# The second residual added with tokens along the partitions, instead of through the down product

## The chip, the cores and the metric

The kernel runs on one core of one Trainium2 chip. The metric is the device time of one execution in microseconds; the figure given for a kernel is the median of its runs. Engines are named as in the profile: PE is TensorE's matrix product, PEld its loading of weights, DVE is VectorE, ACT ScalarE, POOL GpSimd, and SP the queue that issues most DMAs. Each engine works through its own list of instructions in the order in which the program wrote them.

## The reference

The input `x` has 16 sequences of 256 tokens with 128 features, float32. Twelve layers of linear attention (16 heads of 8 features, no softmax) with residuals come first, then two post-norm steps, the second around a gated feed-forward network whose weights are integers times 1/127:

```python
for i in range(12):
    q, k, v = split(x @ Wqkv[i].T + bqkv[i])
    att = einsum('bhqd,bhkd->bhqk', q, k) / sqrt(8)
    x = einsum('bhqk,bhkd->bhqd', att, v) @ Wproj[i].T + bproj[i] + x
x1 = layernorm(x0 + x)                       # x0: the input
gate, up = x1 @ (w_gate / 127).T, x1 @ (w_up / 127).T      # 384 hidden features
out = layernorm(x1 + (silu(gate) * up) @ (w_down / 127).T)
```

`layernorm` takes off the mean and divides by sqrt(variance + 1e-5), with no weights. The change concerns the last line.

## The kernel before

The 16 sequences are worked on as 8 pairs (`p`) of 512 tokens, in two halves of four pairs for the attention. The attention never forms tokens: it carries a 128 x 128 matrix per sequence through the layers and multiplies the tokens by it at the end. Then `ffn(p, prio)` does the rest for one pair:

- `tr_t`, `tr_c`, `mm_r`: the carried matrix is transposed and multiplied with the pair's tokens, which gives `x0 + x` with tokens along the partitions, four chunks of 128 tokens (K = 4) side by side in one PSUM bank.
- `norm(pr, True)`: first norm, from that bank into the SBUF tile `x1` (its memory is that of `kv`, so the profile writes `kv`). The mean is already off; the sum of squares comes from ScalarE (L588) or VectorE (L591, L593).
- `tr_x`: four transposes (L655) bring `x1` into a bank with features along the partitions. There it is split in two parts of reduced precision, `xh` (L657) and the rest `xl` (L658), because products in that precision run faster.
- For each of three blocks of 128 hidden features: gate and up products on `xh` and `xl` (L665, L666), Silu on ScalarE (L668), gate times up on VectorE (L669), the split of the result in `hh` (ScalarE or VectorE) and `hl` (GpSimd or VectorE), and the down products on `hh` and `hl` (L677, L678), which add up in one bank `pd` over the three blocks. `sg0` is written into `xt`, `sg1` into `qgv`.
- The second residual comes in two parts. `xl` enters the bank `pd` as a product with 127 times the identity (`id127r`, L676), and `xh` is added on VectorE as the bank is read: `sg0 = pd / 127 + xh` (L680).
- `tr_o`: four transposes (L684) turn `sg0` back to tokens along the partitions, in bank `po`.
- `norm(po, False)`: second norm, read from that bank. Statistics on VectorE (four L591, four L593), then on GpSimd variance + eps (L600) and its power -0.5 (L601), then `nb` = -mean * rs (L619), then the scaling of four chunks on VectorE (L613) or ScalarE (L615) into the memory of `x1`, and the store (L688). The bank `po` is held until the scaling is done.

Copies, subtractions and casts go through helpers, so many of them have lines L199 (ScalarE), L201 (VectorE or GpSimd) and L204 (subtractions on either).

The order on each engine is not written by hand. Every step is handed to `plan.op(costs, emit, reads, writes, prio)` with a price in ns for each engine that may do it. `Plan.run` is a list scheduler: for every step that is ready it finds the engine on which it would end first, takes the steps that could start earliest, and among these the one with the smallest `prio` less 0.0001 times the price of the longest way that follows it. Pair `p` of the feed-forward part has `prio` 11 + 0.15 p. A step that needs one of the 8 PSUM banks waits until one is free in the plan. So prices decide both the engine and the order. Those that matter here are 69 + n/0.96 for VectorE (n elements per partition), 51 + n/1.2 for ScalarE reading a bank and 94 + n/1.2 reading SBUF, 93 more for each pointer operand; 1276 for the second norm's scaling on VectorE (K * 319); 2.6 N for the store.

At the start, before the plan, GpSimd and VectorE make constants one after another: the identity, masks, `center`, `ones`, and `id127` (L250) with its cast `id127r` (L251). Behind them GpSimd sets the columns of ones beside the loaded tokens (L266), for which TensorE's first products (L329) wait.

Of the kernel before, what the change touches and what calls it, by code (L numbers as in the profile page):

```python
# [9 lines left out]
F32 = mybir.dt.float32  # L10
F32R = mybir.dt.float32r
BF16 = mybir.dt.bfloat16
I32 = mybir.dt.int32
AF = mybir.ActivationFunctionType
ALU = mybir.AluOpType
# [6 lines left out]
C = 128  # L22
# [6 lines left out]
QSCALE = 1.0 / 127.0  # L29
# [5 lines left out]
N = PB * T  # L35
K = N // 128
# [33 lines left out]
PE, ACT, DVE, POOL, SP = "pe", "act", "dve", "pool", "sp"  # L70
# [95 lines left out]
def mmr(n):  # L166
    return max(111, 0.447 * n + 5)


def act(n, sbuf=False, pointers=0):  # L170
    return (94 if sbuf else 51) + 93 * pointers + n / 1.2


def dve(n, fast=False):
    return 69 + n / (1.92 if fast else 0.96)
# [11 lines left out]
def linear_attention_ffn_kernel(ctx: ExitStack, tc: tile.TileContext, x, xt, wall, wq0, bias, wg, wu, wd, out):  # L187
    nc = tc.nc
    sb = ctx.enter_context(tc.tile_pool(name="sb", bufs=1))
    ps = ctx.enter_context(tc.tile_pool(name="ps", bufs=1, space=PSUM))  # L190
    new = lambda name, shape, dt=F32: sb.tile([128, *shape], dt, name=name)
# [3 lines left out]
    bank = lambda v: banks[v.slot]  # L195
# [21 lines left out]
    ident = new("ident", [128])  # L217
# [19 lines left out]
    for g in range(G):  # L237
        rows = slice(32 * g, 32 * g + 32)
# [6 lines left out]
    nc.vector.tensor_copy(centerr, center)  # L245
    ones = new("ones", [C], BF16)
    nc.gpsimd.memset(ones, 1.0)

    id127, id127r = new("id127", [128]), new("id127r", [128], F32R)
    nc.gpsimd.tensor_scalar(id127, ident, 1.0 / QSCALE, 0.0, ALU.mult, ALU.add)  # L250
    nc.vector.tensor_copy(id127r, id127)  # L251


    xts = [new(f"xt{p}", [PB * T]) for p in range(NP)]
    vx = [Val() for _ in range(NP)]
# [287 lines left out]
    vfw = {n: Val() for n in "gud"}  # L543
# [7 lines left out]
    for p in range(NP):  # L551
        t = {f"{n}{j}": new(f"{n}{j}_{p}", [512], F32R) for n in ("hh", "hl") for j in range(NB)}
# [15 lines left out]
    def ffn(p, prio):  # L568
# [8 lines left out]
        def op(costs, emit, reads, writes):  # L577
            plan.op(costs, emit, reads, writes, prio)

        def norm(src, centred):  # L580

            xs, rows = t("x1"), lambda: bank(src)
            cut = lambda a, k: a[:, k * C : (k + 1) * C]

            def stats(e):
                if e == ACT:
                    for k in range(K):
                        nc.scalar.activation(cut(xs, k), cut(rows(), k), AF.Square, scale=1 / math.sqrt(C), accum_out=t("mv")[:, k, 1:2])  # L588
                else:
                    for k in range(K):  # L590
                        nc.vector.bn_stats(t("st")[:, k, :], cut(rows(), k))  # L591
                    for k in range(K):
                        nc.vector.bn_aggr(t("mv")[:, k, :], t("st")[:, k, :])  # L593
            costs = {DVE: K * (dve(C) + 70)}
            if centred:
                costs[ACT] = K * (act(C) + 93)
            op(costs, stats, [src], [v["st"], v["x1"]])

            def rstd(e):
                nc.gpsimd.tensor_scalar(t("ve"), t("mv")[:, :, 1], 1.0, EPS, ALU.mult, ALU.add)  # L600
                nc.gpsimd.tensor_tensor(t("rs"), t("ve"), mhalf, ALU.pow)  # L601
            op({POOL: 1220}, rstd, [v["st"]], [v["rs"]])

            def scale(e):
                if centred and e == DVE:
                    nc.vector.tensor_tensor(chunks(xs), chunks(rows()), t("rs").unsqueeze(2).to_broadcast([128, K, C]), ALU.mult)
                    return
                for k in range(K):
                    d, r, rs = cut(xs, k), cut(rows(), k), t("rs")[:, k : k + 1]
                    if centred:  # L610
                        nc.scalar.activation(d, r, AF.Copy, scale=rs)
                    elif e == DVE:
                        nc.vector.tensor_scalar(d, r, t("mv")[:, k, 0:1], rs, ALU.subtract, ALU.mult)  # L613
                    else:
                        nc.scalar.activation(d, r, AF.Identity, bias=t("nb")[:, k : k + 1], scale=rs)  # L615
            if centred:
                costs = {DVE: dve(N), ACT: K * act(C, False, 1)}
            else:
                op({DVE: 75}, lambda e: nc.vector.scalar_tensor_tensor(t("nb"), t("mv")[:, :, 0], -1.0, t("rs"), ALU.mult, ALU.mult), [v["rs"], v["st"]], [v["nb"]])  # L619
                costs = {DVE: K * 319, ACT: K * act(C, False, 2)}  # L620
            op(costs, scale, [src, v["rs"], v["st"], v["nb"]], [v["x1"]])


        ptt, pc, pr, px, pd, po = (Val("bank") for _ in range(6))
# [34 lines left out]
        for n in range(NH):  # L659
# [12 lines left out]

            def mm_d(e, n=n, hh=hh, hlo=hlo):
                ws = fw["d"][:, n * C : (n + 1) * C]
                if n == 0:
                    nc.tensor.matmul(bank(pd), id127r, t("xl"), start=True, stop=False)  # L676
                nc.tensor.matmul(bank(pd), ws, t(hh), start=False, stop=False)  # L677
                nc.tensor.matmul(bank(pd), ws, t(hlo), start=False, stop=(n == NH - 1))  # L678
            op({PE: (2 + (n == 0)) * mmr(N)}, mm_d, [v[hh], v[hlo], v["xl"], vfw["d"]], [pd])
        op({DVE: dve(N)}, lambda e: nc.vector.scalar_tensor_tensor(t("sg0"), bank(pd), QSCALE, t("xh").bitcast(F32), ALU.mult, ALU.add), [pd, v["xh"]], [v["sg0"]])  # L680

        def tr_o(e):
            for k in range(K):
                nc.tensor.transpose(bank(po)[:, k * C : (k + 1) * C], t("sg0")[:, k * 128 : (k + 1) * 128], ident)  # L684
        op({PE: K * 109}, tr_o, [v["sg0"]], [po])
        norm(po, False)
        r0 = p * N
        op({SP: 2.6 * N}, lambda e: nc.sync.dma_start(out[r0 : r0 + N, :].rearrange("(k p) c -> p k c", p=128), chunks(t("x1"))), [v["x1"]], [])  # L688

# [56 lines left out]
```

## Time and profile before

| | |
|---|---|
| three runs | 313.88, 314.54, 315.0 us; median 314.54 |
| profiled execution | 314.09 us, span from first to last instruction 312.4 us, mean granted TensorE clock 0.986 |
| busy time over the span | PE 297.9 us (95%), DVE 240.1 (77%), ACT 212.4 (68%), POOL 135.4 (43%) |
| chain that ended last | PE 90%, DVE 5%, POOL 2%, DMA 1% |
| first and last start of L676 (8 products of 512 columns) | 266.7 and 297.3 us |
| first and last start of L680 (8, VectorE) | 275.6 and 303.1 us |
| first and last start of L684 (32 transposes) | 279.9 and 304.5 us |
| second norm's scaling | 12 instructions on VectorE (3 pairs), 20 on ScalarE (5 pairs) |
| store of a pair's result | 256 KB, 2.3 us from issue to landing |

Shares over the whole span mix the attention, which lasts until about 254 us, with the feed-forward part behind it, where all that the change moves takes place. The busy time of PE counts a product until its modelled end, and products overlap: the distance from start to start (0.23 us for 512 columns) tells what one costs. The same holds for the four short VectorE or ScalarE instructions of a norm: a row's mean is longer than the distance.

### The profile page before, as it was taken

Reading aid. Unit: us, or ns where it says so; the run is one execution under the profiler, and the core shown is the slowest. Engines: PE = TensorE matmul, PEld = TensorE weight load, DVE = VectorE, ACT = ScalarE, POOL = GpSimd, SP = SyncE. Lnnn points to the kernel's source line nnn. Section 1 sums busy time; section 2 is a strip of 40 time slices with the busy share of each in tenths; the row PEclk is TensorE's granted clock in tenths of the full one; section 3 lists DMA queues with packets and bytes.
Section 4 is the critical chain, followed back from the end, with each engine's and each line's share of the span. In section 5 each row is a group of like instructions: output and inputs, shape, how many; then the busy total and the mean of one; then the engine's idle time right before and its main releaser. Section 6 shows DMA issues by size and latency. Waiting matters only on the chain.

```text
span 312.4 us, 12885 instructions
## 1 busy us (share of the span) xinstructions
PE 297.9 (95%) x5338; PEld 272.9 (87%) x5338; DVE 240.1 (77%) x756; ACT 212.4 (68%) x577; POOL 135.4 (43%) x228
## 2 busy tenths in 40 slices
PE   6989999999999999999999999999999999999970
PEld 6979989999999999999999999999999898888840
DVE  4768887767777677776767777676768798999995
ACT  2448796666767667676686766866876778867651
POOL 6317531445314453144531445312330357568863
PEclk9999999999999999999999999999999999999995
DMA  7473630200202102020120200310000000001124
GB/s 223 110 202 107 187 104 4 65 26 20 69 2 66 26 28 63 2 74 17 30 59 4 64 25 28 81 27 2 4 2 3 5 0 0 2 1 34 37 84 118
DMA packets 22474, 15.66 MB, mean 50 GB/s; under 512 B 1936, under 2 KB 19856, under 8 KB 22416
## 3 DMA queue, kind: packets, MB, share of 16 engines
q1 hardware_dynamic: 22128, 14.75, 17.2%
q8 instruction: 42, 0.69, 0.9%
q14 instruction: 16, 0.13, 0.1%
q10 hardware_dynamic: 288, 0.09, 0.1%
HBM read 8.02 MB, written 2.10 MB: 32 GB/s over the span
## 4 chain that ended last, share of the span: by engine, by line
PE 90%; DVE 5%; POOL 2%; DMA 1%; issue 0%; DVEq 0%; SPq 0%; POOLq 0%
PE bank L456 14%; PE bank L435 8%; PE bank L512 8%; PE bank L437 7%; PE bank L436 6%; PE bank L443 5%; PE bank L500 4%; PE bank L530 4%; PE bank L529 4%; PE bank L531 4%; PE bank L665 3%; PE bank L666 3%; PE bank L444 3%; PE bank L445 3%; PE bank L329 3%; PE bank L649 2%
## 5 line engine op out<-in xcount | busy, mean ns | idle before, releaser
L204 POOL TENSOR_TENSOR thl<-tst,thl 128x260 fp32r<-128x260 f32 x88 | 64.7, 768 | 125.4 <-ACT thl L199 125.4
L199 ACT COPY qgv<-bank 128x256 f32<-128x256 f32 x160 | 56.5, 376 | 22.5 <-PE bank L445 13.3
L199 ACT COPY kv<-bank 128x512 f32<-128x512 f32 (+1 forms) x91 | 51.8, 572 | 21.0 <-PE bank L437 15.1
L435 PE MATMUL bank<-whl,thl 128*128 128x256 f32 x176 | 51.8, 294 | 0.0
L437 PE MATMUL bank<-whl,thl 128*128 128x256 f32 x176 | 49.5, 281 | 0.0
L436 PE MATMUL bank<-whl,thl 128*128 128x256 f32 x176 | 49.4, 281 | 0.0
L456 PE MATMUL bank<-kv,g 128*128 128x128 f32 x352 | 46.3, 275 | 0.0
L536 DVE TENSOR_TENSOR tst<-bank,tst 128x260 f32<-128x260 f32 x96 | 37.0, 424 | 12.0 <-PE bank L531 9.9
L456 PEld LDWEIGHTS bank<-kv,g 128*128 128x128 f32 x352 | 42.9, 191 | 0.2 <-issue 0.2
L199 ACT CAST thl<-tst 128x260 fp32r<-128x260 f32 x88 | 33.1, 408 | 14.5 <-DVE tst L536 14.4
L449 DVE TENSOR_SCALAR qgv<-bank,bcol 128x2 f32<-128x2 f32 x88 | 19.4, 221 | 26.4 <-ACT qgv L199 22.1
L435 PEld LDWEIGHTS bank<-whl,thl 128*128 128x128 f32 x176 | 33.1, 188 | 4.3 <-issue 4.2
L525 DVE TENSOR_TENSOR yhl<-bank,yhl 128x260 fp32r<-128x260 f32 x96 | 34.1, 417 | 0.0
L436 PEld LDWEIGHTS bank<-whl,thl 128*128 128x128 f32 x176 | 33.2, 189 | 0.0
L437 PEld LDWEIGHTS bank<-whl,thl 128*128 128x128 f32 x176 | 33.1, 188 | 0.0
L443 PE MATMUL bank<-thl,whl 128*128 128x260 f32 x88 | 29.1, 330 | 0.0
L512 PE MATMUL bank<-qgv,gm 32*32 32x130 f32 x1536 | 25.8, 280 | 0.7 <-DVE gm L207 0.7
L199 ACT CAST yhl<-bank 128x260 fp32r<-128x260 f32 (+1 forms) x56 | 20.6, 412 | 7.0 <-PE bank L512 5.2
L201 DVE CAST yhl<-bank 128x260 fp32r<-128x260 f32 x48 | 18.3, 423 | 8.9 <-PE bank L512 8.8
L444 PE MATMUL bank<-thl,whl 128*128 128x260 f32 x88 | 24.8, 281 | 0.0
L445 PE MATMUL bank<-thl,whl 128*128 128x260 f32 x88 | 24.7, 280 | 0.0
L512 PEld LDWEIGHTS bank<-qgv,gm 32*32 32x32 f32 x1536 | 17.2, 103 | 6.2 <-DVE gm L207 0.9
(155 smaller groups left out, 717.4 us busy)
## 6 DMA issues: line engine op xcount, KB each, us to landing
wraw<-wall SPq DMA_DIRECT2D x12, 256.0 KB, 3.4
wpt<-whl SPq DMA_DIRECT2D x24, 96.0 KB, 2.2
qgv<-x SPq DMA_DIRECT2D x8, 256.0 KB, 5.2
xt<-xt SPq DMA_DIRECT2D x8, 256.0 KB, 4.4
out<-kv SPq DMA_DIRECT2D x8, 256.0 KB, 2.3
wpt<-whl SPq DMA_DIRECT2D x24, 64.0 KB, 2.8
wpt<-whl SPq DMA_DIRECT2D x24, 32.0 KB, 2.3
wraw<-wg SPq DMA_DIRECT2D x1, 192.0 KB, 2.8
```

Of the source, the lines that this page charges most:

```text
L199: nc.scalar.copy(dst, src)
L204: (nc.vector if e == DVE else nc.gpsimd).tensor_tensor(dst, a, b, ALU.subtract)
L435: nc.tensor.matmul(o, hi[:, b, 0:C], hl(0, 1, 2), start=True, stop=False)
L436: nc.tensor.matmul(o, hi[:, b, 0:C], hl(1, 1, 2), start=False, stop=False)
L437: nc.tensor.matmul(o, lo[:, b, 0:C], hl(0, 1, 2), start=False, stop=True)
L443: nc.tensor.matmul(o, hl(0, 0), flat(hi), start=True, stop=False)
L444: nc.tensor.matmul(o, hl(0, 0), flat(lo), start=False, stop=False)
L445: nc.tensor.matmul(o, hl(1, 0), flat(hi), start=False, stop=True)
L456: nc.tensor.matmul(bank(pgv)[:, b * C : (b + 1) * C], g0[p][:, b, :], tv(b), start=True, stop=True)
L512: nc.tensor.matmul(bank(pys[r])[group(g + r), b * W : (b + 1) * W], gm[group(g), r * PB + b, :], qss[p][group(g), b, :], start=True, stop= ...
L525: plan.op({DVE: dve(PB * W)}, lambda e: nc.vector.tensor_tensor(yl, bank(py)[:, : PB * W], yh.bitcast(F32), ALU.subtract), [py, vyh[p]], [ ...
L536: plan.op({DVE: dve(PB * W)}, lambda e: nc.vector.tensor_tensor(ts, bank(pw)[:, : PB * W], ts, ALU.add), [pw], [vt[p], vc[p]], prio)
```

## The change

The first norm's result `x1` is still in SBUF with tokens along the partitions when the second norm begins. The change adds it there:

- `id127`, `id127r` and the product L676 go; the first down product opens the bank.
- The bank `pd` is read by a scaling alone, `sg0 = pd / 127`, on ScalarE or VectorE by the plan's choice, in the place of L680.
- Behind the transposes a new VectorE addition writes `x1 = po + x1` in place.
- The second norm takes its statistics from `x1` in SBUF, and its scaling reads and writes `x1` there. The bank `po` is free after the addition.
- The prices of that scaling are changed to 4 x 190 = 760 on VectorE and to the SBUF price on ScalarE (4 x 387 = 1547 where it was 4 x 343 = 1373).

The residual is now the unsplit `x1`; the arithmetic is otherwise that of before.

```diff
-    id127, id127r = new("id127", [128]), new("id127r", [128], F32R)
-    nc.gpsimd.tensor_scalar(id127, ident, 1.0 / QSCALE, 0.0, ALU.mult, ALU.add)
-    nc.vector.tensor_copy(id127r, id127)
...
         def norm(src, centred):
-            xs, rows = t("x1"), lambda: bank(src)
+            xs = t("x1")
+            rows = (lambda: bank(src)) if src else (lambda: xs)
+            read = [src] if src else [v["x1"]]
...
-            op(costs, stats, [src], [v["st"], v["x1"]])
+            op(costs, stats, read, [v["st"], *([v["x1"]] if src else [])])
...
-                costs = {DVE: K * 319, ACT: K * act(C, False, 2)}
-            op(costs, scale, [src, v["rs"], v["st"], v["nb"]], [v["x1"]])
+                costs = {DVE: K * 190, ACT: K * act(C, True, 2)}
+            op(costs, scale, [*([src] if src else []), v["rs"], v["st"], v["nb"]], [v["x1"]])
...
             def mm_d(e, n=n, hh=hh, hlo=hlo):
                 ws = fw["d"][:, n * C : (n + 1) * C]
-                if n == 0:
-                    nc.tensor.matmul(bank(pd), id127r, t("xl"), start=True, stop=False)
-                nc.tensor.matmul(bank(pd), ws, t(hh), start=False, stop=False)
+                nc.tensor.matmul(bank(pd), ws, t(hh), start=(n == 0), stop=False)
                 nc.tensor.matmul(bank(pd), ws, t(hlo), start=False, stop=(n == NH - 1))
-            op({PE: (2 + (n == 0)) * mmr(N)}, mm_d, [v[hh], v[hlo], v["xl"], vfw["d"]], [pd])
-        op({DVE: dve(N)}, lambda e: nc.vector.scalar_tensor_tensor(t("sg0"), bank(pd), QSCALE, t("xh").bitcast(F32), ALU.mult, ALU.add), [pd, v["xh"]], [v["sg0"]])
+            op({PE: 2 * mmr(N)}, mm_d, [v[hh], v[hlo], vfw["d"]], [pd])
+        def leave(e):
+            if e == ACT:
+                nc.scalar.activation(t("sg0"), bank(pd), AF.Copy, scale=QSCALE)
+            else:
+                nc.vector.tensor_scalar(t("sg0"), bank(pd), QSCALE, None, ALU.mult)
+        op({ACT: act(N), DVE: dve(N)}, leave, [pd], [v["sg0"]])
...
         op({PE: K * 109}, tr_o, [v["sg0"]], [po])
-        norm(po, False)
+
+        op({DVE: dve(N)}, lambda e: nc.vector.tensor_tensor(t("x1"), bank(po), t("x1"), ALU.add), [po], [v["x1"]])
+        norm(None, False)
```

## The prediction

> **What bounds the kernel now.** I read the page first: the chain that ended last is 90% TensorE and 5% VectorE. Then the chain's last part in order of time, to see where the one hands over to the other:
>
> ```profile
> 293.42 0.23 PE bank L678
> 293.65 0.45 PE bank L684 x4
> 294.10 0.02 issue
> 294.12 0.68 DVE xt L669
> 294.80 0.60 DVE xt L680
> ...
> 303.15 0.60 DVE xt L680
> 303.75 0.80 DVE st L591 x4
> ```
>
> TensorE carries the end until 294.1 us; the last 15 us are VectorE's. Everything the change touches but the set-up lies after 254 us (first gate product). Busy time by stretch (columns: stretch, length, then busy us of PE, PEld, DVE, ACT, POOL, with counts):
>
> ```profile
> 280.00:285.00 5.00, 5.00 (x27) 4.11 (x26) 5.00 (x17) 3.34 (x8) 3.85 (x5) 1.00 0.00 0
> 285.00:290.00 5.00, 5.00 (x27) 4.11 (x25) 4.80 (x16) 4.16 (x11) 4.64 (x5) 1.00 0.19 52
> ...
> 300.00:305.00 5.00, 2.58 (x11) 1.32 (x9) 4.92 (x24) 1.18 (x5) 2.26 (x4) 0.88 0.54 155
> ```
>
> TensorE has no gap before 299, but VectorE has hardly one either: over the stretches from 260 to 300 (9.30 and 9.71 of 10 us, then 5.00, 4.80, 4.83 and 5.00 of 5) it idles 0.70 + 0.29 + 0 + 0.20 + 0.17 + 0 = 1.36 us. In the order of time one pair takes the same 4.85 us on both: output transposes (L684) start at 284.72 and 289.57, and the products L669 that stand at the same place of VectorE's round at 284.60 and 289.45. GpSimd's round (`hl` to `hl`, 284.31 to 289.18) is 4.87 with 0.19 idle. ScalarE alone has room, 0.82 to 0.84 a round. So less TensorE work helps only as far as the others can follow.
>
> **The change part by part.** The profiled execution took 314.09 us (span 312.4, 1.7 around it); the median of the runs is 314.54, 0.45 above. I sum changes and apply them to the median. Prices, from the groups kept apart by shape (mean ns before the last bar):
>
> ```profile
> L658 DVE TENSOR_TENSOR thl<-bank,yhl 128x512 fp32r<-128x512 f32 x8 | 5.5, 682 | 0.8 <-ACT yhl L199 0.8
> ...
> L680 DVE SCALAR_TENSOR_TENSOR xt<-bank,yhl 128x512 f32<-128x512 f32 x8 | 5.4, 677 | 0.0
> ...
> L613 DVE TENSOR_SCALAR kv<-bank,mv,rs 128x128 f32<-128x128 f32 x12 | 4.1, 400 | 0.0
> ...
> L676 PE MATMUL bank<-thl,id127r 128*128 128x512 f32 x8 | 3.4, 425 | 0.0
> ```
>
> *Set-up.* L250 on GpSimd and L251 on VectorE go. The chain runs through L250 (4.66) to the memsets (4.90) that release TensorE's first product at 5.06, so 0.24 us comes out. Bounds: 0, should the input's landing then be last, and 0.30 (the row's duration). L251 (0.80) goes at nothing: VectorE then waits 1.40 for TensorE.
>
> *The pass of 127 times the identity.* Matmuls of this shape start 0.23 us apart, so eight passes are 1.85 us of TensorE. Those at 293.84 and 297.29 lie behind the hand-over; six count, 1.39. What is late next is VectorE, with 1.36 idle, then GpSimd. Bounds 0 and 1.36. I take half, 0.70: fewer products do not speed GpSimd's round, but the two hh casts and hl subtractions a round that can sit on either of two engines can shift.
>
> *Leaving the bank.* The residual add on VectorE (677 ns, 0.60 to the next start) becomes a scaling of one input on ScalarE or VectorE. ScalarE's nearest row is the Silu of the same shape, 602 to 608 ns, 0.50 apart: eight are 4.0, inside its room of 0.82 a round. If that cover is gone it costs VectorE 0.60 a pair. Waiting for the last down product, it holds up Silu passes queued behind it on ScalarE, as the add held up products on VectorE.
>
> *The new add.* A bank and an SBUF tile in, 512 wide: L658's shape, 682 ns, 0.60 apart. It is 8 x 0.60 against the 8 x 0.60 removed: VectorE's load is level where the leaving goes to ScalarE. It waits for the transposes as the statistics did, with those statistics and later pairs' products behind it. It frees the transposes' bank after one operation instead of after the last scaling (289.57 to 299.1 for the third pair); I count that at nothing, because TensorE shows no wait for a bank; the bounds are 0 and what the plan makes of it.
>
> *Statistics from SBUF.* Nearest rows: 278 ns from a bank (L591), 274 for a reduction of 128x128 in SBUF (L289). Nothing.
>
> *Scaling from SBUF.* On VectorE four take 1.36 now (400 ns each, 0.32 apart, so 80 ns overlap). The one row in SBUF of the kind, L291, is 286 ns: 0.206 apart, 0.90 for four. The bounds are 0.62 (L201's 128x128 cast, 216 ns) and 1.36; I take 0.90, the same kind of instruction. [...] On ScalarE four take 1.50 now (L615); the nearest pair of rows (622 ns from SBUF, 603 from a bank) leaves that as it is.
>
> *The drain.* VectorE is packed from 294.12 to 306.13. There five adds stand where four L680 stood (+0.60), and the fifth pair's scaling shrinks (1.28 to 0.90, -0.38): +0.22. The last scaling, alone after the last GpSimd power, shrinks 1.36 to 0.90: -0.46. Together -0.24; bounds -0.80 (0.62 for both) and +0.60 (no shrinking). The last pair's own chain trades L680 on VectorE for ScalarE, and does not wait behind a scaling from 301.76 to 303.08; VectorE's load hides that gain. The store behind it is unchanged.
>
> Sum: -0.24 - 0.70 - 0.24 = -1.18, from 314.54 to 313.4. With every gain at its end: -0.30 - 1.36 - 0.80 = -2.46, 312.1.
>
> **The rivals.**
>
> *Level: VectorE and GpSimd keep the round at 4.85.* For: both are full, and an order fixed in advance rarely uses the last tenth. Against: one of three hh casts in the round is VectorE's by choice, and ScalarE has room. The pass's 0.70 is lost: -0.24 - 0.24 = -0.48, 314.1; one leaving left on VectorE makes it 314.7.
>
> *Slower: scalings move to VectorE and meet GpSimd.* Today five of eight pairs are scaled by ScalarE. The planner's prices were 1276 against 1373 ns; they become 760 against 1547. One 512-wide operation queued on VectorE (602) used to send the scaling to ScalarE and now will not. In SBUF it then competes with GpSimd, as the order of time shows for a cast of 128x512 in SBUF:
>
> ```profile
> 289.11 0.43 DVE L201 CAST hh<-xt 128x512 fp32r<-128x512 f32 x1
> ...
> 290.64 2.55 POOL L204 TENSOR_TENSOR hl<-xt,hh 128x512 fp32r<-128x512 f32 x2
> ...
> 292.63 0.84 DVE L201 CAST hh<-qgv 128x512 fp32r<-128x512 f32 x1
> ```
>
> The same cast takes 0.43, or 0.84 when it starts within a GpSimd subtraction; and a subtraction with such a cast beside it takes 1.50 to 1.53 instead of 1.30. [...] I use the 0.41 of the rows: each moved scaling costs VectorE 0.90 + 0.41 = 1.31. One fits in the idle 1.36; two make 2.62 - 1.36 - 0.48 = +0.78, still level; three decide: 3.93 - 1.36 - 0.48 = +2.1, 316.6. Against it: the planner lets later pairs' products pass a scaling, and when two have passed it the scaling goes to ScalarE after all.
>
> That the change does not do what it says can only be in part: the pass is gone in any case, but which engine leaves and scales is the planner's choice. That is in the two rivals.
>
> **How the numbers follow.** About 0.3%, 0.94 us, is what a measurement of this kernel can tell from no change. The first case (313.4, own range 312.1 to 313.6) gets 0.42: set-up and last scaling are near certain, and half of the pass's idle is enough. Level gets 0.32, three or more scalings on VectorE in the full stretch 0.26. Outside 312.1 to 316.0 I leave 0.04 below and 0.14 above, about half of the slow case.
>
> **What would show it.** Right: no L676; first TensorE product near 4.8 instead of 5.06; rounds of 4.6 to 4.75 us between output transposes; the leaving mostly on ScalarE at 0.5 to 0.6; the add near 680 ns; four SBUF scalings in 0.9 or less; VectorE's packed stretch ending about 1 us earlier. The set-up term is wrong if the first product stays at 5.06; the middle term if rounds stay at 4.85; the drain if the last scaling takes over 1.2. The whole is wrong if three or more of the five scalings that ScalarE does now are VectorE's, with single ones stretched to over 0.6 beside GpSimd's subtractions.

## The result and the profile after

| kernel | median us | range | ratio to before, 95% interval |
|---|---|---|---|
| before | 314.57 | 313.48 to 315.0 | 1 |
| after | 317.22 | 316.85 to 317.87 | 1.0091 [1.0073, 1.0108] |

The change makes the kernel 2.65 us slower by the medians; the ratios here and below are of mean times. The forecast was 313.4 with a range up to 316.0, so it was wrong in sign. After's profiled execution took 316.96 us (span 315.2, 1.8 around it), and the comparisons below use it.

The share of the chain that ended last, by engine, was 90% TensorE and 5% VectorE before. After:

```profile
PE 88%; DVE 8%; POOL 1%; DMA 1%; issue 0%; POOLq 0%; DVEq 0%
```

The last part of that chain in order of time (start, length, what):

```profile
289.55 0.24 PE bank L672
289.83 0.43 DVE hh L201
290.26 0.60 DVE kv L687
290.86 1.45 DVE hl L204
292.31 0.60 DVE qgv L666
292.91 0.78 DVE st L588 x4
...
296.34 0.59 DVE nb L616
296.94 0.78 DVE st L588 x4
...
300.19 0.60 DVE hl L204
300.79 1.17 DVE nb L616
301.96 0.78 DVE st L588 x4
...
311.12 0.77 DVE kv L610 x3
```

The hand-over from TensorE to VectorE, at 294.1 before, now comes at 289.8, and VectorE carries the last 22 us where it carried 15. Three entries are odd. `nb` works on 128x4 elements, yet stands in the chain with 0.59 and 1.17 us; one `hl` of 128x512, 0.60 elsewhere, stands with 1.45. Before, `nb` took (mean ns before the last bar):

```profile
L619 DVE SCALAR_TENSOR_TENSOR nb<-mv,rs 128x4 f32<-128x4 f32 x8 | 1.3, 162 | 0.1
```

Busy time by stretch (columns: stretch, length, then busy us of PE, PEld, DVE, ACT, POOL, with counts):

```profile
280.00:285.00 5.00, 5.00 (x26) 4.08 (x25) 4.96 (x15) 4.43 (x8) 3.98 (x5) 1.00 0.00 0
285.00:290.00 5.00, 5.00 (x25) 4.11 (x24) 5.00 (x18) 2.82 (x6) 2.29 (x4) 1.00 0.18 52
...
295.00:300.00 5.00, 2.80 (x16) 1.75 (x14) 5.00 (x18) 1.98 (x5) 2.84 (x4) 1.00 0.01 1
300.00:305.00 5.00, 2.29 (x12) 1.48 (x12) 5.00 (x19) 3.80 (x10) 2.76 (x3) 1.00 0.26 74
305.00:313.00 8.00, 0.00 (x0) 0.00 (x0) 6.49 (x38) 2.31 (x6) 3.67 (x6) 0.56 0.57 155
```

TensorE's saving is there: it is idle 2.2 us of 295 to 300, where it had none before, and the output transposes (L684) come every 4.60 us (278.80, 283.40, 288.01) instead of every 4.85. But nothing is gained by that: VectorE is full from 285 to 305, and TensorE waits for the leavings on ScalarE, which stand behind casts that wait for VectorE's products (0.83 and 2.19 us of 295 to 300). The last transposes start at 304.18 instead of 303.81. Counted from the same point of the work, 28 us ahead of the first output transposes, to the end, VectorE is busy 58.94 us instead of 55.34 (251.87 on before, 250.80 on after). That is 3.60 more; from those transposes to VectorE's last instruction it takes 33.09 us instead of 29.18, 3.91 more. They start 1.07 earlier, so 2.84 of the 3.91 stay at the end (311.89 against 309.05), close to the 2.65 lost.

The groups by line, kept apart by shape (busy, mean ns of one, idle before):

```profile
L610 DVE TENSOR_SCALAR kv<-kv,mv,rs 128x128 f32<-128x128 f32 x20 | 6.6, 394 | 0.0
...
L687 DVE TENSOR_TENSOR kv<-bank,kv 128x512 f32<-128x512 f32 x8 | 5.4, 681 | 0.0
...
L677 ACT ACTIVATE xt<-bank 128x512 f32<-128x512 f32 x8 | 4.7, 593 | 0.0
...
L204 DVE TENSOR_TENSOR hl<-qgv,hh 128x512 fp32r<-128x512 f32 x4 | 3.6, 896 | 0.0
...
L616 DVE SCALAR_TENSOR_TENSOR nb<-mv,rs 128x4 f32<-128x4 f32 x8 | 3.0, 372 | 0.4 <-POOL rs L598 0.4
```

VectorE now scales five pairs (20 instructions) and ScalarE three; before it was three and five. VectorE has 11 `hl` subtractions instead of 9, and 6 `hh` casts instead of 9. All eight leavings are ScalarE's, and the new addition costs what it was said to (681 ns).

The order of time on VectorE, the stretched instructions alone:

```profile
283.99 2.18 DVE L610 TENSOR_SCALAR kv<-kv,mv,rs 128x128 f32<-128x128 f32 x4
...
290.77 1.54 DVE L204 TENSOR_TENSOR hl<-qgv,hh 128x512 fp32r<-128x512 f32 x1
...
296.26 0.67 DVE L616 SCALAR_TENSOR_TENSOR nb<-mv,rs 128x4 f32<-128x4 f32 x1
...
300.71 1.26 DVE L616 SCALAR_TENSOR_TENSOR nb<-mv,rs 128x4 f32<-128x4 f32 x1
```

and on GpSimd in the same stretch:

```profile
284.00 1.30 POOL L204 TENSOR_TENSOR hl<-xt,hh 128x512 fp32r<-128x512 f32 x1
...
290.47 3.00 POOL L204 TENSOR_TENSOR hl<-xt,hh 128x512 fp32r<-128x512 f32 x2
...
295.62 1.30 POOL L204 TENSOR_TENSOR hl<-xt,hh 128x512 fp32r<-128x512 f32 x1 [0.28 <-ACT hh L199]
...
300.38 1.56 POOL L204 TENSOR_TENSOR hl<-xt,hh 128x512 fp32r<-128x512 f32 x1 [1.01 <-ACT hh L199]
```

Each long `nb` ends with a GpSimd subtraction: 296.26 + 0.67 = 296.93 against 295.62 + 1.30 = 296.92, and 300.71 + 1.26 = 301.97 against 300.38 + 1.56 = 301.94. I call *stretched time* what `hl`, `hh`, `nb` and the scalings from SBUF take on VectorE above their undisturbed durations in these traces (0.69, 0.43, 0.15 and 1.10 for four; in a run of several, 0.60, 0.34, 0.07 and 0.27 for each further one). It is 1.12 us before and 3.73 after; it depends on these base values to about 0.1.

### The profile page after: what moved, and what is told of

Read it like the earlier page. It is cut to its first block, busy times and chain, and to the rows that moved or that the text cites. A ratio compares the mean times of both kernels' runs of the same rounds, so it can differ in the third digit from the quotient of the medians.

```text
span 315.2 us, 12881 instructions
## 1 busy us (share of the span) xinstructions
PE 295.7 (94%) x5330; PEld 270.7 (86%) x5330; DVE 242.6 (77%) x762; ACT 215.5 (68%) x580; POOL 131.2 (42%) x225
## 4 chain that ended last, share of the span: by engine, by line
PE 88%; DVE 8%; POOL 1%; DMA 1%; issue 0%; POOLq 0%; DVEq 0%
PE bank L451 14%; PE bank L430 8%; PE bank L507 8%; PE bank L432 6%; PE bank L431 6%; PE bank L438 5%; PE bank L495 4%; PE bank L525 4%; PE bank L524 4%; PE bank L526 3%; PE bank L662 3%; PE bank L439 3%; PE bank L440 3%; PE bank L663 3%; PE bank L324 3%; PE bank L646 2%
```

## The experiments

Three theories were set against each other. *Load*: VectorE is the bound, and the plan's price of 190 ns gave it more work than it had. *Lock*: VectorE's operations between SBUF operands wait for GpSimd's subtractions. *Chain*: the added step behind the transposes makes every pair's end late. Times are medians; the ratio is to runs of before on the same chip (there its medians were 314.1 to 314.3). An interval that takes in 1 does not tell a run from before; I call that level. *VectorE busy* is from 28 us ahead of the first output transposes to the end, *tail* from those transposes to VectorE's last instruction; both come from one profiled execution each, as does the stretched time. That execution lies up to 1.1 us from the run's median (e11, which reached the feed-forward part 1.25 late).

| run | ratio, 95% | median | on VectorE: scalings / hl / hh | VectorE busy | tail | stretched |
|---|---|---|---|---|---|---|
| before | 1 | | 3 / 9 / 9 | 55.34 | 29.18 | 1.12 |
| after | 1.0091 [1.0073, 1.0108] | 317.22 | 5 / 11 / 6 | 58.94 | 33.09 | 3.73 |
| e1_old_prices | 1.0014 [0.9997, 1.0031] | 314.71 | 3 / 11 / 4 | 56.49 | 30.64 | 3.34 |
| e2_scale_act | 1.0019 [0.9998, 1.0040] | 314.57 | 0 / 13 / 4 | 53.66 | 28.81 | 2.22 |
| e3_nb_pool | 1.0032 [1.0013, 1.0052] | 315.39 | 3 / 12 / 5 | 55.73 | 30.76 | 2.01 |
| e4_pass_only | 1.0016 [0.9995, 1.0036] | 315.01 | 2 / 11 / 8 | 56.56 | 30.38 | 3.03 |
| e5_port_after | 1.0045 [1.0025, 1.0065] | 316.05 | 4 / 12 / 5 | 57.52 | 31.66 | 2.27 |
| e6_port_before | 1.0027 [1.0013, 1.0042] | 315.03 | 3 / 11 / 7 | 56.21 | 30.02 | 1.94 |
| e7_port_price | 1.0027 [1.0004, 1.0050] | 315.26 | 3 / 12 / 5 | 56.84 | 30.98 | 2.07 |
| e9_setup | 0.9985 [0.9972, 0.9998] | 313.82 | 3 / 9 / 9 | 55.25 | 29.16 | 1.13 |
| e10_before_old_plan | 0.9999 [0.9986, 1.0012] | 314.23 | 3 / 9 / 9 | 55.40 | 29.63 | 1.30 |
| e11_after_old_plan | 1.0047 [1.0031, 1.0063] | 315.50 | 3 / 9 / 9 | 55.91 | 31.13 | 1.84 |
| e12_sum_in_bank | 0.9985 [0.9971, 0.9999] | 313.75 | 3 / 11 / 4 | 55.22 | 29.07 | 1.22 |
| e13_bank_cheap | 1.0102 [1.0079, 1.0125] | 316.95 | 5 / 11 / 6 | 59.48 | 33.28 | 2.81 |
| e15_bank_hldear | 0.9977 [0.9959, 0.9994] | 313.55 | 2 / 7 / 4 | 53.85 | 28.77 | 1.81 |

**The old price.** The scaling's price in the plan goes back to that of before; nothing else changes.

```diff
-                costs = {DVE: K * 190, ACT: K * act(C, True, 2)}
+                costs = {DVE: K * 319, ACT: K * act(C, False, 2)}
```

> The changed kernel with the second norm's scaling priced as before (1276 on VectorE, 1373 on ScalarE); the two scalings that moved to VectorE (first and fourth pair) go back to ScalarE. Load theory (the loss is VectorE's extra work, at a price the planner has too low): two scalings of 1.08 us off VectorE, 317.2 - 2.2 = 315.0. Lock theory (the loss is VectorE waiting behind GpSimd's subtractions for operands that both lie in SBUF): the one stretched scaling (2.18 us) and a plain one go, about -3.2 at most, but the stretched nb and hl stay; 314.5 to 316. Chain theory (the added step behind the transposes makes the end late, whoever scales): within 0.5 of 317.2.

The price is worth 1.0091 − 1.0014 = 0.77% (± 0.25% from the two intervals) of the 0.91%, or 2.4 us. VectorE's busy time falls by 2.45 and its tail by 2.45. The parts give that: two scalings fewer (2 x 1.03), two `hh` fewer (2 x 0.34), one leaving more (0.60), 0.39 less stretched, 2.53 together. The stretched time hardly falls, so here the price acts through the load. Load had 315.0 and Lock 314.5 to 316, so the time itself (314.71) does not tell these two apart. The added step is still there, so Chain is no cause of a loss of this size.

**The scaling on ScalarE alone.**

```diff
-                costs = {DVE: K * 190, ACT: K * act(C, True, 2)}
+                costs = {ACT: K * act(C, True, 2)}
```

> The changed kernel with all eight second-norm scalings on ScalarE. Load theory: five scalings, 5.4 us, off VectorE, of which the last costs ScalarE 1.65 instead of 1.1 at the end: 313 to 315. Lock theory: only the stretched scaling's 1.1 us and what follows it: 315.5 to 316.5, with nb still up to 1.2 us long beside a subtraction. Chain theory: no faster than 316.7, because the last pair's chain gets 0.55 longer.

VectorE is busy 5.3 us less than in after, but the time is 314.57, level with before, because the end is now ScalarE's. Load's 313 to 315 holds; Lock and Chain had it later. Its chain's last part:

```profile
299.11 1.65 ACT kv L612 x4
300.75 0.48 ACT xt L677
301.24 5.79 ACT kv L612 x15
```

Fifteen scalings in a row are on the path. So the scalings cannot all go there either.

**`nb` on GpSimd.** In rstd, two GpSimd operations (a scaling by −1, a product with `rs`) make `nb`, and VectorE's operation goes.

```diff
+                if not centred:
+                    nc.gpsimd.tensor_scalar(t("nb"), t("mv")[:, :, 0], -1.0, 0.0, ALU.mult, ALU.add)
                 nc.gpsimd.tensor_tensor(t("rs"), t("ve"), mhalf, ALU.pow)
+                if not centred:
+                    nc.gpsimd.tensor_tensor(t("nb"), t("nb"), t("rs"), ALU.mult)
-            op({POOL: 1220}, rstd, [v["st"]], [v["rs"]])
+            op({POOL: 1220 if centred else 1620}, rstd, [v["st"]], [v["rs"]] if centred else [v["rs"], v["nb"]])
```

> The changed kernel with nb (minus mean times rs) made by GpSimd right behind the power instead of by VectorE. Lock theory: the two nb that took 1.26 and 0.67 us on VectorE beside a subtraction (1.17 and 0.59 on the chain against 0.1 for a free one) leave it, -1.5, and GpSimd's two small operations add about 0.4 to the last chain: 316.0 to 316.3. Load theory: eight nb of 0.1 are 0.8 less on VectorE, 0.4 more at the end: 316.8 to 317.2. Chain theory: 317.2 to 317.6.

The time falls to 0.32% above before (315.39), below what any theory forecast, but the run differs from after in its plan too: the planner now gave VectorE three scalings. Without `nb` on VectorE one scaling takes the meeting instead (3.06 us for four, at 284.58). Which operation is stretched depends on the order; in each of the fifteen kernels of the table some are, by 1.1 to 3.7 us in all.

**The pass alone.** Before, without L676.

```diff
-                if n == 0:
-                    nc.tensor.matmul(bank(pd), id127r, t("xl"), start=True, stop=False)
-                nc.tensor.matmul(bank(pd), ws, t(hh), start=False, stop=False)
+                nc.tensor.matmul(bank(pd), ws, t(hh), start=(n == 0), stop=False)
```

> The kernel before with nothing but the pass of 127 times the identity left out; this leaves out the low part xl of the residual. It measures what TensorE's 1.85 us are worth with VectorE's work as before. If VectorE is the bound with 1.36 us idle from 260 to 300: -0.3 to -1.4, half of it, 0.7, as the prediction's middle term. If TensorE's rounds shorten but the drain takes it back: 0 to -0.3.

The time is level with before, so neither half of the expectation (−0.3 to −1.4, 0 to −0.3) is borne out: TensorE's 1.85 us are worth nothing here. The first rounds shrink as in after, and VectorE's stretched time grows to 3.03.

**A planner that keeps the pair apart.** The planner of after, then of before, does not let VectorE's operations between SBUF operands overlap a GpSimd `hl` in its own reckoning.

```diff
+        held_until = 0.0
...
-                    t = max(free[e], held)
+                    t = max(free[e], held, held_until if e in o.pair else 0.0)
...
+            if e in o.pair:
+                held_until = end
```

> The changed kernel; only the planner differs: it now also keeps apart in time VectorE's operations with both operands in SBUF (hl, hh, nb, the SBUF scaling) and GpSimd's hl subtractions, as if they shared one resource. VectorE gets 4 scalings, 12 hl and 5 hh (5, 11 and 6 in the changed kernel). Lock theory: of the some 3.7 us in which VectorE's rows are stretched beside subtractions, two thirds go: 314.5 to 315.5. Load theory: -1.08 + 0.60 - 0.34 = -0.8, 316.4. If only the order of the end matters: no forecast, 316 to 318.

> The kernel before with the same addition to its planner (VectorE: 3 scalings as before, 11 hl for 9, 7 hh for 9). Lock theory: there is little to win, its rows are stretched by some 0.9 us in all: 0 to -0.5. Load theory: + 1.2 - 0.7 = +0.5.

The third of them adds a price of 265 ns to the first, near the 0.26 that one scaling from SBUF takes in a run.

```diff
-                costs = {DVE: K * 190, ACT: K * act(C, True, 2)}
+                costs = {DVE: K * 265, ACT: K * act(C, True, 2)}
```

> The changed kernel with that planner and the SBUF scaling priced at 4 x 265 on VectorE, the 1.08 us that its trace shows, instead of 4 x 190 (3 scalings, 12 hl, 5 hh on VectorE). Lock and load theories together: -2 for the stretching and -1.5 for two scalings with one hl more and one hh less: 313.5 to 314.5. Load theory alone: 315.4 to 315.9.

None is faster than before. The planner's times are not the chip's, so meetings remain (2.27, 1.94, 2.07 us stretched), and to before itself the constraint costs 0.27%, where Lock had a small gain and Load +0.5 us. With the price of 265 VectorE scales three pairs again and after goes from 0.45% to 0.27% above before; the intervals overlap, so that step is not shown. Its 315.26 is slower than Load and Lock together had it (314.5 at most).

**Lock by itself.** After, with a stretch of its own behind the last scaling: one round each of VectorE operations, three times alone and four times behind the start of 20 GpSimd subtractions of 128x512 back to back; its total time means nothing. GpSimd ended at 358.03, so three of the four rounds lie beside it and the fourth, from 358.11, is alone again.

```diff
+            nc.vector.tensor_tensor(bo, ba, bb, ALU.subtract)
+            nc.vector.tensor_tensor(bo, bk, bb, ALU.add)
+            nc.vector.scalar_tensor_tensor(bn[:, i, :], bs[:, :, 0], -1.0, bs[:, :, 1], ALU.mult, ALU.mult)
...
+        for _ in range(19):
+            nc.gpsimd.tensor_tensor(bp, ba, bb, ALU.subtract)
```

> The changed kernel with a stretch added behind the last scaling that measures the disputed cost by itself, on tiles no longer needed: on VectorE, three times alone and four times beside a row of 20 GpSimd subtractions of 128x512 in SBUF, a subtraction of two SBUF tiles, an addition of a bank and an SBUF tile, nb, four scalings from SBUF, four from a bank and four statistics from SBUF. Its own time means nothing. [...] If GpSimd merely shares bandwidth: all of them some 10 to 30% longer, none by a whole subtraction. Alone the four SBUF scalings take 1.1.

VectorE's order of time, a round alone, then a round beside GpSimd:

```profile
320.49 0.15 DVE L730 SCALAR_TENSOR_TENSOR bench_n<-bench_s 128x4 f32<-128x4 f32 x1
320.60 1.12 DVE L732 TENSOR_SCALAR xt<-xt,bench_s 128x128 f32<-128x128 f32 x4
321.63 1.36 DVE L734 TENSOR_SCALAR xt<-bank,bench_s 128x128 f32<-128x128 f32 x4
322.91 0.86 DVE L736 BATCH_NORM_STATS2 bench_st<-xt 128x6 f32<-128x128 f32 x4
...
332.87 0.69 DVE L729 TENSOR_TENSOR xt<-bank,xt 128x512 f32<-128x512 f32 x1
333.48 0.50 DVE L730 SCALAR_TENSOR_TENSOR bench_n<-bench_s 128x4 f32<-128x4 f32 x1
333.90 4.22 DVE L732 TENSOR_SCALAR xt<-xt,bench_s 128x128 f32<-128x128 f32 x4
338.04 1.36 DVE L734 TENSOR_SCALAR xt<-bank,bench_s 128x128 f32<-128x128 f32 x4
339.32 0.86 DVE L736 BATCH_NORM_STATS2 bench_st<-xt 128x6 f32<-128x128 f32 x4
```

Four scalings from SBUF take 4.22 instead of 1.12, 3.1 us more, a little over two of the subtractions (27.0 us for 19, 1.42 each); the same scalings from a bank, the sum from a bank and an SBUF tile, and the statistics from SBUF take what they take alone. `nb` goes from 0.15 to 0.50 in all three rounds. The subtraction of two SBUF tiles starts at 331.71 in the first round, inside a GpSimd subtraction, and takes 1.13 instead of 0.69; in the other two (340.80 and 349.46) it takes 0.69, though GpSimd's 19 subtractions last from 331.03 to 358.03. After's trace shows which of the two engines waits. VectorE's `hl` of 300.11 takes 0.68, and the GpSimd subtraction that starts inside it, at 300.38, takes 1.56 instead of 1.30; the `nb` of 300.71, which starts inside that subtraction, takes 1.26 and ends with it. There the one that started later waited. So the waiting that Lock supposes is measured, and it is not every SBUF operand that meets it.

**The set-up alone.** Before, with L250 and L251 put behind the memsets of L266.

```diff
-    nc.gpsimd.tensor_scalar(id127, ident, 1.0 / QSCALE, 0.0, ALU.mult, ALU.add)
-    nc.vector.tensor_copy(id127r, id127)
...
     for p in range(NP):
         nc.gpsimd.memset(xtoks[p][:, :, C:], 1.0)
...
+    nc.gpsimd.tensor_scalar(id127, ident, 1.0 / QSCALE, 0.0, ALU.mult, ALU.add)
+    nc.vector.tensor_copy(id127r, id127)
```

> The kernel before, with the two instructions that make 127 times the identity (GpSimd, VectorE) put behind the memsets that release TensorE's first product; the plan is untouched. All theories: the first product starts near 4.8 instead of 5.06 us, every later step 0.25 to 0.3 us earlier, 314.2 becomes 313.9 (ratio 0.999). If the end does not move with the first product, the set-up term of the prediction is wrong.

The first product starts at 4.77, and the median falls by 0.44 (0.06 to 0.88 by the interval). This term of the sum stands, though only just clear of nothing: the profiled execution (314.33, among the four slowest of twelve) does not show the gain at its end, since its first output transposes start at 280.13, 0.26 later than before's.

**The pass, in before's order.** Before without the passes and their set-up, planned as if they were there.

```diff
-    nc.gpsimd.tensor_scalar(id127, ident, 1.0 / QSCALE, 0.0, ALU.mult, ALU.add)
-    nc.vector.tensor_copy(id127r, id127)
...
-                if n == 0:
-                    nc.tensor.matmul(bank(pd), id127r, t("xl"), start=True, stop=False)
...
             op({PE: (2 + (n == 0)) * mmr(N)}, mm_d, [v[hh], v[hlo], v["xl"], vfw["d"]], [pd])
```

> The kernel before without the eight passes of 127 times the identity and without their set-up, but planned as if the passes were still there: every other instruction keeps its engine and its place. Left out: xl's share of the second residual. It differs from the earlier run without the passes only in the plan. Load: VectorE's work is that of before, so the set-up's 0.28 and 0.2 to 1.36 us of VectorE's idle time come off: 312.6 to 313.7, ratio 0.995 to 0.9985. Lock: the same if the stretched operations (1.05 us of excess before) stay at or under 1.1 us; with TensorE ahead, other operations can meet GpSimd's subtractions, and each 0.5 us of further excess eats 0.5 us; above 2.4 us it is level. A new plan is not the cause if this kernel is no faster than 314.7.

Every other instruction has its old engine and place, and the stretched time is 1.30, yet the time is level with before, and no better than the set-up alone (0.9985 against 0.9999). Load and Lock, which both had it at 313.7 or less, missed. The chain shows where the saving goes:

```profile
286.06 0.23 PE bank L662
286.29 0.25 PE bank L663
286.54 0.66 ACT hh L199
```

TensorE hands over at 286.5 instead of 294.1, 7.6 us earlier, and the work of ScalarE, GpSimd and VectorE from there to the end takes as much longer: VectorE's busy time (55.40) is that of before. VectorE's own round stays too: its product (L666 here, L669 before) starts at 284.62 and 289.50, 4.88 apart, where before had 4.85. From the first norm's scaling that waits for GpSimd (260.73 before) to VectorE's last instruction it is 48.32 us before and with the set-up alone, and 48.08 here: about 0.24 us of the 1.85 come through in these traces, and none that can be told in the medians. A new plan is therefore not needed to lose the saving.

**The whole change, in before's order.** After's instructions at the places of before's: the leaving (on ScalarE) where the residual addition stood, the addition ahead of its statistics.

```diff
-            op({PE: 2 * mmr(N)}, mm_d, [v[hh], v[hlo], vfw["d"]], [pd])
+            op({PE: (2 + (n == 0)) * mmr(N)}, mm_d, [v[hh], v[hlo], v["xl"], vfw["d"]], [pd])
...
-        op({ACT: act(N), DVE: dve(N)}, leave, [pd], [v["sg0"]])
+        op({DVE: dve(N)}, lambda e: leave(ACT), [pd, v["xh"]], [v["sg0"]])
...
+                    if not centred:
+                        nc.vector.tensor_tensor(xs, bank(src), xs, ALU.add)
                     for k in range(K):
                         nc.vector.bn_stats(t("st")[:, k, :], cut(rows(), k))
```

> The kernel after in the order of before: planned with the operations and prices of before, each new instruction put in the place of the old one (the leaving, on ScalarE, where the residual addition stood in the plan; the addition just ahead of its statistics; four scalings from SBUF where those from the bank stood, three pairs on VectorE and five on ScalarE). It computes all that after computes. The prediction's sum would give -1.18: 313.0, ratio 0.996. Load: VectorE has 3 x 0.25 = 0.75 us less work than before, less the set-up's 0.28: 312.8 to 313.6. Lock: the same less what three scalings that now read SBUF lose; 313.0 to 314.0 with an excess of 1 to 2 us, level with before if all three meet a subtraction (up to 1.1 us each). Chain: the addition behind the transposes makes each pair's end late whatever the plan: 315.5 or more.

It is 0.47% slower than before, a miss for Load and Lock and just Chain's number (315.5). Its profiled execution is the slowest of its seven (316.61): it enters the feed-forward part 1.25 late, and from the first norm's scaling on it takes 1.26 us more than before. VectorE is busy only 0.57 us more and 1.84 us are stretched, but the tail is 1.95 longer. Between 285 and 290 VectorE idles 0.78, and the two engines' order of time shows on what. ScalarE first:

```profile
285.75 1.64 ACT L613 ACTIVATE kv<-kv,nb,rs 128x128 f32<-128x128 f32 x4
287.29 0.58 ACT L678 ACTIVATE xt<-bank 128x512 f32<-128x512 f32 x1
287.77 0.59 ACT L666 ACTIVATE xt<-bank 128x512 f32<-128x512 f32 x1
288.24 0.62 ACT L199 CAST hh<-xt 128x512 fp32r<-128x512 f32 x1
```

then VectorE:

```profile
288.90 0.69 DVE L204 TENSOR_TENSOR hl<-xt,hh 128x512 fp32r<-128x512 f32 x1 [0.74 <-ACT hh L199]
```

The leaving takes 0.49 on ScalarE ahead of the Silu and the cast that VectorE's `hl` waits for (in before's kernel without the passes that wait is 0.23). So a step added ahead of others does make the end late, as Chain has it, but in this place it is the leaving, not the addition, in an order that knows nothing of it. Of the 1.26 us, VectorE idles 0.98 (0.54 more ahead of this `hl`, 0.30 more ahead of the last `nb`, which waits for GpSimd) and is busy 0.28 more.

**The sum written back into the bank.** After with the old prices and one more difference: VectorE writes the second residual's sum into the transposes' bank, and statistics and scaling read the bank as before.

```diff
-        op({DVE: dve(N)}, lambda e: nc.vector.tensor_tensor(t("x1"), bank(po), t("x1"), ALU.add), [po], [v["x1"]])
-        norm(None, False)
+        op({DVE: dve(N)}, lambda e: nc.vector.tensor_tensor(bank(po), bank(po), t("x1"), ALU.add), [po, v["x1"]], [po])
+        norm(po, False)
```

> The kernel after, with the second residual's sum written back into the transposes' bank, so that statistics and scaling read the bank as before and have the prices of before; VectorE has 3 scalings, 11 hl and 4 hh, as in the run of after with the old prices, but the scalings read no SBUF operand of full width. Load: against that run (314.71, ratio 1.0014) 3 x 0.25 = 0.75 us more work: 315.3, ratio 1.0035. Lock: the scalings cannot be stretched, the excess falls from 3.35 to about 2.2 us: 313.6 to 314.5, ratio 0.998 to 1.001. Chain: as after, 317 or more.

It is Lock's number. Engines and order are those of the run with the old price, and only the place of the sum differs. Against that run the gain is 0.29% (± 0.22%), though three scalings cost 0.25 more each; the stretched time falls from 3.34 to 1.22, VectorE's busy time by 1.27 (2.12 less 0.75 is 1.37), its tail by 1.57. The freed scaling itself is 1.06 of the 2.12; the rest are an `nb` and an `hl` that met a subtraction in the one run and not in the other, as the times shifted. To before, 0.9985 is no more than the set-up alone gives (0.9985).

**The same with after's price.** The edit of the sum's place as above, the prices left as in after (`K * 190`).

> The kernel after with the sum written back into the transposes' bank, but with after's prices: each engine has after's instructions in after's order, VectorE five scalings, 11 hl and 6 hh; only the place of the sum differs. Load (each VectorE operation costs its own time): 5 x 0.25 = 1.25 us more than after, 318.4, ratio 1.013. Lock, where only the scalings are freed: 1.25 more and the one stretched scaling's 1.09 less, 317.4, ratio 1.0095; where nb and hl lose their meetings too as the order in time shifts, up to 2.6 us less again, 314.8, ratio 1.002. If it comes out at 313.8 like the run with the sum in the bank and the old prices, the price did nothing and the place of the sum is the whole cause.

Each engine has after's instructions in after's order, and only the place of the sum differs. The time is level with after (1.0102 against 1.0091), so with after's prices the place of the sum is worth nothing within ± 0.29%: the one stretched scaling's 1.08 is gone, and five scalings from the bank cost 5 x 0.25 more. VectorE's groups:

```profile
L610 DVE TENSOR_SCALAR kv<-bank,mv,rs 128x128 f32<-128x128 f32 x20 | 6.8, 402 | 0.0
...
L616 DVE SCALAR_TENSOR_TENSOR nb<-mv,rs 128x4 f32<-128x4 f32 x8 | 3.2, 398 | 0.1
```

The price alone, now with no scaling that could be stretched, costs 1.0102 − 0.9985 = 1.17% (± 0.27%), 3.7 us. Two scalings more are 2 x 1.28, two `hh` 2 x 0.34, one leaving less −0.60: 2.64. With 1.59 more stretched, by `nb` above all (0.86 at 294.61, 1.25 at 299.52), that makes 4.23; VectorE's busy time rose by 4.26, its tail by 4.21. So the larger part of what the price costs is Load, in both places of the sum.

**Less on VectorE.** The sum in the bank, the old prices, and `hl` on VectorE priced at 1.5 times.

```diff
-            op({POOL: pool(N), DVE: dve(N)}, lambda e, sg=sg, hh=hh, hlo=hlo: sub(e, t(hlo), t(sg), t(hh).bitcast(F32)), [v[sg], v[hh]], [v[hlo]])
+            op({POOL: pool(N), DVE: 1.5 * dve(N)}, lambda e, sg=sg, hh=hh, hlo=hlo: sub(e, t(hlo), t(sg), t(hh).bitcast(F32)), [v[sg], v[hh]], [v[hlo]])
```

> The run with the sum in the bank and the old prices (313.75), with hl on VectorE priced at 1.5 times in the plan: VectorE has 7 hl instead of 11, 2 scalings instead of 3, 2 leavings instead of 1; GpSimd has 17 hl instead of 13. Load: VectorE has 4 x 0.60 + 1.28 - 0.60 = 3.1 us less; GpSimd 4 x 1.3 = 5.2 more, in rounds where it had 1 us and more idle: 312.0 to 313.4, ratio 0.993 to 0.997, the end going to VectorE after the last products. Lock: fewer hl of VectorE to be stretched but more subtractions to meet; 312.5 to 313.7. If it is slower than 314.3, GpSimd's round, not VectorE, sets the end.

VectorE's busy time falls by 1.37 (it also got one more scaling of the first norm, which the expectation did not count), the tail by 0.30, the median by 0.20 to 313.55. That is in Lock's range (312.5 to 313.7) and just short of the 313.4 that Load wanted; the step from 313.75 is not clear of noise. VectorE alone no longer holds the end: it idles 1.13 us of 270 to 280. This version, 0.9977 [0.9959, 0.9994], and the one with the sum in the bank and the old prices, 0.9985, are faster than both kernels, to before by 0.23% and 0.15%; their intervals come within 0.06% and 0.01% of no change, and the set-up alone gives as much as the second.

## Why the prediction was wrong

*Set-up, −0.24.* Right as far as it can be told: −0.28 at after's first product, −0.44 in the time of the set-up alone, the interval (0.06 to 0.88) taking in the forecast.

*The pass, −0.70.* Wrong, and this step failed first. With order and engines held, the kernel without the pass is 0.14% ± 0.18% slower than the one with the set-up alone moved, and 0.24 us shorter in this part of their traces: little or nothing of the 0.70. The saving on TensorE was real, rounds of 4.60 as forecast. But the step took VectorE's idle 1.36 us for room. It is not: a gap in a fixed order belongs to what the engine waits for there. The two longest waits of before's 260 to 300 are not for TensorE:

```profile
260.73 0.69 DVE L606 TENSOR_TENSOR kv<-bank,rs 128x512 f32<-128x512 f32 x1 [0.46 <-POOL rs L601]
...
287.15 0.69 DVE L204 TENSOR_TENSOR hl<-xt,hh 128x512 fp32r<-128x512 f32 x1 [0.20 <-ACT hh L199]
```

With two shorter ones (0.14 and 0.12 us) the `hl` wait 0.45 for ScalarE's casts. Only 0.17 us, ahead of two products L669 (at 269.51 and 291.91), end with a matrix product. Without the pass these two gaps are gone and the other four are still there:

```profile
261.02 0.69 DVE L603 TENSOR_TENSOR kv<-bank,rs 128x512 f32<-128x512 f32 x1 [0.45 <-POOL rs L598]
...
287.21 0.72 DVE L204 TENSOR_TENSOR hl<-xt,hh 128x512 fp32r<-128x512 f32 x1 [0.23 <-ACT hh L199]
```

The Level rival had this right: VectorE's rounds stayed (4.88), and only TensorE's became shorter.

*Leaving, hidden on ScalarE at 0.50.* All eight were there, at 593 ns. Hidden holds only where the plan knows of it; in before's order it pushed a cast back by 0.49, and VectorE with it.

*The addition, level.* Right: 681 ns, 0.60 apart. *Statistics from SBUF, nothing.* Right: 277 ns.

*Scaling from SBUF, 0.90 for four.* Mis-sized: 1.08 to 1.11, 0.26 apart, free of GpSimd. SBUF against bank is 1.11 against 1.36 (to the next instruction's start, 1.03 against 1.28). The plan's price (760 for four) was too low by some 0.3 us.

*The drain, −0.24.* Wrong, with the opposite sign. The last scaling did shrink, from 1.36 to 1.11. But the drain began 4.3 us earlier and carried more: VectorE's last statistics ended at 309.2 instead of 306.1, where the forecast had the packed stretch end 1 us earlier.

*What the sum left out.* It kept before's three scalings on VectorE and gave the plan's new prices nothing; it had them in a rival alone. The plan moved two, and that is worth 2.4 us (the run with the old price): the larger part of the miss.

*The Slower rival* named the mechanism, and its trigger came in half: two scalings moved, not three. It then let 1.36 us of idle time pay for them, for +0.78 with the gain of the drain beside it, where 2.65 came. Without that room its own price of 1.31 for each gives 2.62, and 2.4 less the set-up; but this nearness is partly chance. It charged the meetings with GpSimd to the moved scalings only. In after just one of five scalings met a subtraction (+1.08); `nb`, of 128x4 elements, lost 1.80 and one `hl` 0.85, which the prediction did not look at. And the two moved scalings came with two more `hl` and three fewer `hh`.

On the waiting itself after's trace and the separate stretch agree: `nb` waits to the very end of a subtraction in the one (1.26 us long, 1.17 of it in the chain), and in the other four scalings beside subtractions lose 0.78 each of subtractions of 1.42. The 0.41 of before's rows, which the rival used, was a cast that started late in a subtraction (at 292.63, where that ended at 293.19): a chance value of one meeting, not a price.

So the cause of the loss is shown in two steps: the cheap price puts two more scalings on a VectorE that has no room (2.4 us with the sum in SBUF, 3.7 in the bank), and with the old price, operands in SBUF cost 0.9 us (0.2 to 1.6) against the same sum in the bank. With the cheap price the place of the sum makes no difference that can be told. Against before, after's VectorE has 5 x 1.03 − 3 x 1.28 = 1.31 us more of scalings, 1.20 of `hl`, 1.02 less of `hh`, and 2.61 more stretched: 4.10, where its busy time rose by 3.60 and its tail by 3.91. Reckoned from before, then, the stretched time is the larger share, and reckoned from the old price the load is: how the loss divides between Load and Lock depends on the kernel that one starts from. What is not settled is why a given order meets GpSimd where another does not: `nb` is stretched by 1.8 to 2.0 us in both runs with the cheap price and by 0.7 and 0.2 with the old one. Nor was the leaving's place on ScalarE tried by itself, apart from the run in before's order; in after VectorE is full from 285 to 305 all the same.

## What to carry to other kernels

Idle time that an engine has in a fixed order is not room: find what each gap waits for, and count a saving on the bound engine at nothing unless that is sped up too. When a plan chooses engines by price, recompute the choice under the new prices before summing; a price 30% too low (760 against 1080 for four) for an engine that was full cost 2.4 us, more than the 1.85 that the removed products had taken on TensorE. Where GpSimd works beside VectorE, even an operation of 128x4 between SBUF operands can cost most of a GpSimd instruction (`nb` took 1.26 us here instead of 0.15, beside a subtraction of 1.56); operations that read one operand from a bank did not meet it here (0.69 for 128x512, 1.36 for four scalings, beside subtractions as alone).

## What had not been expected of the hardware

Not every VectorE operation on SBUF waits for GpSimd. Beside back-to-back subtractions, four scalings from SBUF went from 1.12 to 4.22 us and `nb` from 0.15 to 0.50, while the statistics from SBUF stayed at 0.86, and all forms with a bank as an operand stayed as they were (0.69 and 0.67, four scalings 1.36). Nor does every meeting cost VectorE: a subtraction between two SBUF tiles took 1.13 instead of 0.69 when it started inside a GpSimd subtraction, and 0.69 in the other two rounds. In after it was GpSimd's subtraction that took 1.56 instead of 1.30, where VectorE's `hl` had started first (300.11 against 300.38). A scaling of 128x128 from SBUF is only 0.06 us faster than from a bank (0.26 against 0.32 apart).
